# Two graph layers on one core: head projection by seven block products for each pair of node tiles, adjacency in six parts per tile

## The chip, the cores and the metric

The kernel runs on one core of one Trainium2 chip. The metric is the device time of one execution in microseconds. Five engines are named as the profile names them: PE (matrix multiply; PEld is its weight load), DVE (vector), ACT (scalar), POOL and SP (here mostly issuers of transfers).

## The reference

A graph with 3327 nodes and 1024 features per node goes through two layers. Between the two stands a residual sum and a layer norm, and the second layer begins with a projection of every node onto eight heads of 64 features.

```
h = relu(layernorm(x));  x = x + gnn0(h, adj)     # adj @ quantised(relu(quantised(h) @ quantised(w)))
h = relu(layernorm(x));  x = x + gnn1(h, adj)

def gnn1(x, adj):
    Wh = einsum('nf,hfd->hnd', x, W)              # the projection of the heads: [3327 x 1024] @ [1024 x 512]
    e_src, e_dst = Wh . a1, Wh . a2
    att = softmax(where(adj > 0, leaky_relu(e_src + e_dst), -9e15))
    h = elu(att @ Wh)
    return mlp(h)                                 # four dense layers
```

## The kernel before

The nodes are padded to T = 26 tiles of 128. The kernel runs through stages. Stage 1 makes the quantised support `s_int` of the first layer. Stage 2 multiplies the adjacency by it and prepares the second layer for each node tile. Stage 3 is the attention (masks, selections, sums), and stage 4 the dense layers. The change lies in stage 2.

**What stage 2 does for one tile t.** The transposed adjacency of the tile, 26 blocks of 128 by 128, comes in from memory in four parts of 7, 6, 7 and 6 blocks (`SUBS`, used as `PARTS`, lines 47 and 48). For each part the function `adjacency` (line 177) loads `at` (L186, on SP's queue), lets ACT round it to `hi` (L190), lets DVE take the rest as `lo` (L194), and lets DVE write the mask bytes `mk` (L195). There are three buffers for `at`, and two each for `hi` and `lo`; a buffer of `hi` or `lo` comes free when PE has finished the part that used it two parts before. Then PE multiplies each block of `hi` and of `lo` by the support block, in two matmuls of 512 columns each (L723), so a block takes four matmuls and a tile 104. All of them add up in one pair of PSUM banks, `mm`.

When a tile is summed, what follows is called its **row chain** here: ACT scales `mm` into `y` (L738), DVE scales it again (L739), adds the residual row `xt` (L740) and takes the layer norm (L146 to L151); ACT writes two halves `yh` (L616), two transposing transfers turn them (L618, on SP's queue), and ACT joins them to `ht` (L622), the transposed rows of the tile.

**The heads.** `heads(t, ht, r)` (line 645) multiplies `ht` by the head weights `whead` in eight full-precision matmuls of 512 columns (L652), which the profile records as sixteen. ACT takes the sum out of PSUM as `wht` (L659). What comes after that is called the **closing** of a tile here: DVE multiplies and reduces `wht` for both attention vectors (L666, L667), writes two small tables (L670, L671), ACT takes exponentials (L672, L692), DVE scales `ft` (L693, twice), ACT casts `ft` to `fw` (L697), DVE subtracts (L698), ACT casts again (L699), DVE subtracts again (L700), and POOL's queue sends `fw` to memory as `feat_d` (L703). `wht`, `prod`, `ft` and `fw` have one buffer each.

**The order.** In the loop at line 709 the heads of tile t - 1 are called ahead of the last part of tile t. The next part's `adjacency` is always traced one part ahead, at the moment PE's matmuls of a part are traced. So in the text of the program the closing of tile t - 1 stands before the row chain of tile t, and that stands before the casts of parts 1, 2 and 3 of tile t + 1. A scheduler puts the instructions of each engine in order when the program is built; `keep_in_program_order` fixes an instruction behind the one traced before it on its engine, `issue_after` fixes a transfer behind another. The transfer of a tile's first part is issued after the transposes of the tile two before it. The heads of the last two tiles are taken after the loop (line 760 and on), where the attention has begun.

The attention scores of the sources are collected in `srcs` and sent out in batches after the tiles named in `BATCHES` (line 50).

Of the kernel before, what the change touches and what calls it, by code (L numbers as in the profile page):

```python
# [8 lines left out]
F32 = mybir.dt.float32  # L9
# [37 lines left out]
SUBS = [range(0, 7), range(7, 13), range(13, 20), range(20, 26)]  # L47
PARTS = SUBS
GROUPS = [(0, 1), (2, 3), (4, 5), (6,), (7, 8), (9, 10), (11, 12)]
BATCHES = {12: 0, T - 3: 13}  # L50
GT = 2
# [15 lines left out]
def two_layer_kernel(  # L67
# [105 lines left out]
    with tc.tile_pool(name="at", bufs=2, reuse_waits="tile") as atp:  # L173
# [3 lines left out]
        def adjacency(t, js, mk, turned):  # L177

            nj = len(js)
            r = slice(js[0], js[0] + nj)  # L180
            at = atp.tile([P, 7, P], F32, tag="at", name="at", bufs=3)[:, :nj]
            if mk is None:
                mk = atp.tile([P, T + 2, P], U8, tag="mk", name="mk")[:, :T]

            with tc.issue_after(turned.ins) if js is PARTS[0] and turned is not None else nullcontext():
                ins = nc.sync.dma_start(at, adj_t[t][:, r, :])  # L186
            if t == 0:
                tc.keep_in_program_order(ins)
            hi = atp.tile([P, 7, P], F32R, tag="hi", name="hi")[:, :nj]
            ins = nc.scalar.copy(hi, at)  # L190
            if t == 0:
                tc.keep_in_program_order(ins)
            lo = atp.tile([P, 7, P], F32R, tag="lo", name="lo")[:, :nj]
            nc.vector.tensor_tensor(lo, at, hi.bitcast(F32), ALU.subtract)  # L194
            ins = nc.vector.tensor_scalar(mk[:, r], at, 0.0, float(EDGE), ALU.is_gt, ALU.mult)  # L195
            if t == 0:
                tc.keep_in_program_order(ins)
            if js is PARTS[-1]:
                if t == T - 1:
                    nc.vector.memset(mk[:, :, rows_of(t) :], EDGE)  # L200
                nc.gpsimd.dma_start(mask_d[t], mk)
            return hi, lo, mk
# [389 lines left out]

        with tc.tile_pool(name="wh", bufs=1, reuse_waits="tile") as whp, tc.tile_pool(
            name="s2", bufs=2, reuse_waits="tile"
# [5 lines left out]

            whead = whp.tile([P, KF, EMB], F32, name="whead")
            a1_t = whp.tile([P, EMB], F32, name="a1_t")
            a2_t = whp.tile([P, EMB], F32, name="a2_t")

            joins, planes = [], []

            def transposed_by_dma(y):


                ht = s2.tile([P, KF, P], F32, name="ht", bufs=1)  # L610
                parts = []
# [18 lines left out]

            def transposed_by_tensor(y):

                ht = s2.tile([P, KF, P], F32, name="ht", bufs=1)
                ends, copies = [], []
                for g in range(KF // 4):
                    tp = last_ps.tile([P, 4, P], F32, tag="last", name="tp2")
                    turns = [
                        nc.tensor.transpose(tp[:, q, :], y[:, (4 * g + q) * P : (4 * g + q + 1) * P], ident)
                        for q in range(4)
                    ]  # L640
                    ends.append((turns[0], turns[-1]))
                    copies.append(nc.scalar.copy(ht[:, 4 * g : 4 * g + 4, :], tp))
                return ht, ends, copies

            def heads(t, ht, r, own=None):
                if t == T - 1:
                    whm = last_ps.tile([P, EMB], F32, tag="last", name="whm")
                else:
                    whm = wh_ps.tile([P, EMB], F32, name="whm")
                of_k, products, own_lows, own_ups = [], [], [], []  # L650
                for k in range(KF):
                    ins = nc.tensor.matmul(  # L652
                        whm, ht[:, k, :], whead[:, k, :], start=(k == 0), stop=(k == KF - 1)
                    )
                    of_k.append(ins)
                    if k == 0 and t < T - 1:
                        tc.keep_in_program_order(ins)
                wht = s2.tile([P, EMB], F32, name="wht", bufs=1)
                ins = taken = nc.scalar.activation(wht, whm, AF.Copy, scale=r)  # L659
                if t < T - 2:  # L660
                    tc.keep_in_program_order(ins)
                src = srcs[:, t]
# [10 lines left out]
                if t in BATCHES:  # L673
# [5 lines left out]
                    )  # L679
                    srct = s2.tile([P, P], F32, name="srct")  # L680
                    nc.scalar.copy(srct[:n], sp[:n, :P])
# [9 lines left out]
                for q, slope in enumerate((1.0, SLOPE)):  # L691
                    powers.append(nc.scalar.activation(ft[:, :, q, HD], dst, AF.Exp, scale=slope))  # L692
                    scaled = nc.vector.tensor_tensor(  # L693
                        ft[:, :, q, :HD], wh3, ft[:, :, q, HD:].to_broadcast([P, NH, HD]), ALU.mult
                    )
                fw = s2.tile([P, NH, 2, 3, HC], BF16, name="fw", bufs=1)
                highs = nc.scalar.copy(fw[:, :, :, 0], ft)  # L697
                nc.vector.tensor_tensor(ft, ft, fw[:, :, :, 0], ALU.subtract)  # L698
                nc.scalar.copy(fw[:, :, :, 1], ft)  # L699
                lows = nc.vector.tensor_tensor(fw[:, :, :, 2], ft, fw[:, :, :, 1], ALU.subtract)  # L700
                if own is not None:
# [3 lines left out]
                )  # L705
                return of_k, products, lows, powers, highs, taken

            before = None
            for t in range(T):
                xt = s2.tile([P, F], F32, name="xt2")  # L710

                with tc.issue_after(turned.ins) if turned is not None else nullcontext():
                    load_rows(xt, x, t)
                mm = mm_ps.tile([P, F], F32, tag="mm", name="mm2")
                for js in PARTS:
                    hi, lo = part
                    part = next(columns, None)
                    if js is PARTS[-1] and before is not None and t < T - 1:
                        heads(*before)
                    for q, j in enumerate(js):  # L720
                        for which in (hi, lo):
                            for c in range(FC):
# [5 lines left out]
                                    stop=(j == T - 1 and which is lo),  # L728
                                )
                if t == 0:  # L730
                    for dst, ap in (
# [13 lines left out]
                if t == T - 1:  # L745
                    break
                ht, turned = transposed_by_dma(y)
                before = t, ht, r
            supp.close()
# [9 lines left out]

            of_k, products, _, powers, _, taken = heads(*before, own=f_even)  # L760
            queue_behind(products[0], lacking)
            queue_behind(taken, lacking)
            ht, turns, copies = transposed_by_tensor(y)
            queue_behind(copies[0], taken)
# [504 lines left out]
```

## Time and profile before

| what | us |
|---|---|
| median of 3 runs | 2133.86 (2132.22 to 2136.22) |
| the profiled execution | 2132.73 |
| its span in the profile | 2131.0 |
| PE busy in the span | 2096.3 (98%) |
| DVE busy / ACT busy | 1395.4 (65%) / 1343.1 (63%) |
| matmuls of the heads (L652), busy | 182.7 |
| matmuls of the adjacency (L723, hi and lo), busy | 426.3 + 416.8 |

The span is what the profiler sees from the first to the last instruction; the execution took 1.7 us more. Busy times of matmuls overlap, since matmuls are pipelined; the pace of PE is read from the starts, not from these sums. The stretch from about 127 to 899 us is stage 2, from about 983 to 1838 us the attention runs without a break, and the dense layers follow.

In one full tile of stage 2 (564.99 to 595.44 us, 30.45 us long) PE is busy 30.45 us, DVE 17.66 and ACT 15.66.

### The profile page before, as it was taken

What the parts mean: (1) busy time and instruction counts of PE and PEld (TensorE: products, weight loads), DVE (VectorE), ACT (ScalarE), POOL (GpSimd) and SP (SyncE); (2) the same over time, 40 slices, a digit from 0 to 9 for tenths busy, and PEclk for the clock granted to TensorE, in tenths of its full rate; (3) what the DMA queues carried; (4) which work ended last, traced back from release to release, by engine and by line L of the source; (5) the groups of instructions that cost most, each with busy time, mean ns of one, the idle gap of its engine ahead of it and who ended that gap; (6) DMA issues with size and microseconds to landing.
All of it is one profiled execution on the core that took longest, in us unless ns stands there. A gap on an engine that the chain in (4) does not pass through costs nothing.

```text
span 2131.0 us, 36616 instructions
## 1 busy us (share of the span) xinstructions
PE 2096.3 (98%) x15099; PEld 1689.4 (79%) x15109; DVE 1395.4 (65%) x2568; ACT 1343.1 (63%) x1748; POOL 160.7 (8%) x250
## 2 busy tenths in 40 slices
PE   5999999999999999999999999999999999999999
PEld 2467777777777777779999999999999999844444
DVE  8845566556655665577777777777777777655446
ACT  6734454545454545579888888888888888742321
POOL 2300000000200000200000000000000000000000
PEclk9999999999999999999999999999999999999999
DMA  6654544454455444691202012120202104443322
GB/s 219 173 167 142 161 135 147 150 162 135 146 153 161 133 146 153 173 325 26 74 17 74 22 43 57 26 67 21 74 25 75 26 17 132 111 117 119 113 85 74
DMA packets 184088, 233.22 MB, mean 109 GB/s; under 512 B 103924, under 2 KB 132164, under 8 KB 183920
## 3 DMA queue, kind: packets, MB, share of 16 engines
q1 hardware_dynamic: 168684, 176.91, 27.7%
q0 software_dynamic: 15168, 53.90, 8.2%
q8 instruction: 118, 1.93, 0.4%
q14 instruction: 50, 0.41, 0.1%
q10 hardware_dynamic: 68, 0.06, 0.0%
HBM read 141.21 MB, written 66.02 MB: 97 GB/s over the span
## 4 chain that ended last, share of the span: by engine, by line
PE 92%; ACT 2%; DVE 2%; DMA 2%; issue 2%; SPq 0%; POOL 0%; DVEq 0%; POOLq 0%; ACTq 0%
PE acc L875 41%; PE mm L723 28%; PE whm L652 8%; PE o L1179 7%; PE h_ps L1111 5%; PE mm L342 3%; ACT over L846 1%; DMA feat_d<-fw 1%; PE h_ps L1037 1%; DMA xqt<-xq 0%; DMA w<-in_w 0%; DVE stats L255 0%; ACT xb L314 0%; DMA xt<-in_x 0%; DVE w_stats L385 0%
## 5 line engine op out<-in xcount | busy, mean ns | idle before, releaser
L875 PEld LDWEIGHTS <-sel 128*128 128x128 fp8e4 x10816 | 932.1, 97 | 5.9 <-issue 4.6
L846 ACT ACTIVATE over<-srow,large_dst 128x896 uint8<-128x896 f32 (+1 forms) x766 | 684.4, 975 | 30.0 <-DVE sel L855 30.0
L875 PE MATMUL acc<-f_even,sel 128*128 128x195 bf16 x5408 | 468.2, 248 | 0.6 <-DVE su L894 0.5
L875 PE MATMUL acc<-f_odd,sel 128*128 128x195 bf16 x5408 | 467.4, 247 | 0.0
L723 PE MATMUL mm<-s_int,hi 128*128 128x512 f32 x1352 | 426.3, 396 | 0.0
L723 PE MATMUL mm<-s_int,lo 128*128 128x512 f32 x1352 | 416.8, 390 | 0.0
L855 DVE TENSOR_TENSOR sel<-over,mask 128x448 uint32<-128x448 uint32 (+1 forms) x416 | 243.9, 586 | 216.4 <-ACT over L846 115.2
L723 PEld LDWEIGHTS mm<-s_int,hi 128*128 128x128 f32 x1352 | 254.0, 188 | 62.3 <-issue 11.5
L723 PEld LDWEIGHTS mm<-s_int,lo 128*128 128x128 f32 x1352 | 253.8, 188 | 52.8
L856 DVE TENSOR_TENSOR sel<-sel,mask 128x448 uint32<-128x448 uint32 (+1 forms) x416 | 246.0, 591 | 14.2
L190 ACT CAST hi<-at 128x896 fp32r<-128x896 f32 x104 | 92.4, 888 | 152.9 <-PE mm L723 73.3
L652 PE MATMUL whm<-whead,ht 128*128 128x512 f32 x416 | 182.7, 592 | 0.0
L195 DVE TENSOR_SCALAR mk<-at 128x896 uint8<-128x896 f32 (+1 forms) x104 | 59.5, 590 | 172.9 <-DMA at<-in_adj_t 172.8
L194 DVE TENSOR_TENSOR lo<-at,hi 128x896 fp32r<-128x896 f32 x104 | 106.2, 1021 | 68.1 <-ACT hi L190 68.1
L652 PEld LDWEIGHTS whm<-whead,ht 128*128 128x128 f32 x416 | 78.9, 190 | 89.0 <-issue 87.1
L923 POOL DMA_DIRECT2D enc_d<-eh x64 | 57.7, 905 | 860.4 <-ACT eh L921 859.8
L908 ACT ACTIVATE ht<-su,rs 128x64 f32<-128x64 f32 x208 | 53.1, 335 | 108.7 <-DVE rs L904 108.7
L894 DVE TENSOR_REDUCE su<-acc 128x130 f32<-128x390 f32 x208 | 115.7, 556 | 7.9 <-PE acc L875 7.9
L1121 ACT ACTIVATE h<-h_ps,rest 128x512 f32<-128x512 f32 (+1 forms) x52 | 33.7, 654 | 118.7 <-PE h_ps L1111 118.7
L342 PE MATMUL mm<-w_int,xqt 128*128 128x512 bf16 x406 | 93.9, 385 | 6.8 <-DVE w_int L473 4.5
L659 ACT ACTIVATE wht<-whm,lnr 128x512 f32<-128x512 f32 x26 | 17.8, 685 | 119.3 <-PE whm L652 104.5
L622 ACT COPY ht<-yht 128x1024 uint16<-128x1024 uint16 x50 | 67.4, 1356 | 32.3 <-DMA yht<-yh 32.1
(189 smaller groups left out, 1683.5 us busy)
## 6 DMA issues: line engine op xcount, KB each, us to landing
at<-in_adj_t SPq DMA_DIRECT2D x52, 448.0 KB, 4.7
feat_d<-fw POOLq DMA_DIRECT2D x26, 780.0 KB, 6.5
at<-in_adj_t SPq DMA_DIRECT2D x52, 384.0 KB, 4.0
x_d<-xt POOLq DMA_DIRECT2D x26, 512.0 KB, 2.9
nodes<-x_d SPq DMA_DIRECT2D x26, 512.0 KB, 4.9
xt<-in_x SPq DMA_DIRECT2D x25, 512.0 KB, 4.0
out<-yo SPq DMA_DIRECT2D x50, 256.0 KB, 2.0
xs<-in_x SPq DMA_DIRECT2D x24, 512.0 KB, 4.5
```

The lines of the kernel that those rows point to most:

```text
L190: ins = nc.scalar.copy(hi, at)
L194: nc.vector.tensor_tensor(lo, at, hi.bitcast(F32), ALU.subtract)
L342: nc.tensor.matmul(mms[t][:, r], xqts[t][:, k, :], w_int[:, k, r], start=(k == 0), stop=(k == KF - 1))
L652: ins = nc.tensor.matmul(whm, ht[:, k, :], whead[:, k, :], start=(k == 0), stop=(k == KF - 1))
L723: nc.tensor.matmul(mm[:, c * 512 : (c + 1) * 512], which[:, q, :], s_int[j][:, c * 512 : (c + 1) * 512], start=(j == 0 and which is hi), s ...
L846: nc.scalar.activation(over[:, q], srows[i], AF.Relu, bias=large_dst[:, j, h : h + 1], scale=BIG)
L855: pin(nc.vector.tensor_tensor(up, over, of_pair, ALU.bitwise_and))
L856: ends["vector"] = pin(nc.vector.tensor_tensor(dn, up, of_pair, ALU.bitwise_xor))
L875: ins = nc.tensor.matmul(accs[i, b][:, r], chosen[i, pair][:, s, b, q], f[:, j, r], start=(j == 0 and s == 0), stop=(j == T - 1 and s == 1),)
L894: nc.vector.tensor_reduce(su[:, b], accs.pop((i, b)).rearrange("p (q s c) -> p q c s", q=2, s=3), AX.X, ALU.add)
L1111: ins = nc.tensor.matmul(pss[m][:, :cols], wt[:, k, m * P : (m + 1) * P], xt[:, k, :cols], start=(k == 0), stop=(k == k_n - 1),)
L1179: nc.tensor.matmul(ps, st[:, k, q // 2], mv[:, k], start=(k == 0), stop=(k == 1))
```

## The change

For 24 of the 26 tiles the projection is taken for two tiles at once. The rows of the two tiles are seen as a 2 by 2 matrix of blocks (tile, half of the features), the weights as a 2 by 2 matrix of blocks (half of the features, half of the heads). The product of the two is formed from seven products of blocks instead of eight, with sums and differences of blocks before and after. Each block product is four matmuls of 256 columns.

- `weight_differences` makes three difference blocks and overwrites the block `b12` of `whead`; it runs once, in tile 1. Near the end `b12` is loaded again for the last two tiles, which still use eight products.
- `combined` forms the sums and differences of the rows of a pair, in four DVE instructions of 512 columns. It runs in every even tile t from 2 on, for tiles t - 2 and t - 1.
- `pair_of_heads` is a generator: it runs in the last part of that even tile, and puts the products between the four blocks of that part: products 1 and 2, block, 6 and 3, block, 7 and 5, block, 4, block. ACT copies the first product, DVE adds up the others, and then the closings of both tiles follow, one after the other. In odd tiles there is no projection.
- The old closing becomes the function `closing_of_heads`; its instructions are the same.
- The adjacency of a tile comes in six parts of 5, 5, 4, 4, 4 and 4 blocks. The buffers of `at`, `hi` and `lo` keep their numbers (3, 2, 2) and shrink from seven blocks to five.
- `ht` gets two buffers by name (`ht0`, `ht1`). `xt2` goes from two buffers to one. The combined rows use the buffers of `y` and `prod`; `srct` uses that of `prod`. The batches of source scores close one tile later and at the same last tile as before (`BATCHES`).

```
-PARTS = SUBS
+PARTS = [range(0, 5), range(5, 10), range(10, 14), range(14, 18), range(18, 22), range(22, 26)]
+PN = len(PARTS[0])
-BATCHES = {12: 0, T - 3: 13}
+BATCHES = {13: 0, T - 3: 14}
...
+            def weight_differences():
+                for d, one, other in ((t3, b22, b12), (b12, b12, b11), (t2, b22, b12), (t4, b21, t2)):
+                    nc.vector.tensor_tensor(d, one, other, ALU.subtract)
+
+            def combined(t):
+                (a11, a12), (a21, a22) = halves(t), halves(t + 1)
...
+                nc.vector.tensor_tensor(s1, a21, a22, ALU.add)
+                nc.vector.tensor_tensor(s2_, s1, a11, ALU.subtract)
+                nc.vector.tensor_tensor(a21, a11, a21, ALU.subtract)
+                nc.vector.tensor_tensor(s4_, a12, s2_, ALU.subtract)
...
+            def pair_of_heads(t, of):
+                r0, r1 = scales.pop(t), scales.pop(t + 1)
+                wht = s2.tile([P, EMB], F32, name="wht", bufs=1)
...
+                def product(b):
+                    st, mv = of[b]
+                    if b in "1674":
+                        banks.append(wh_ps.tile([P, 2, EMB // 2], F32, name="products"))
+                    ps = banks[-1][:, b in "235"]
+                    for k in range(KF // 2):
+                        order(
+                            nc.tensor.matmul(ps, st[:, k], mv[:, k], start=(k == 0), stop=(k == KF // 2 - 1))
+                        )
+                    return ps
...
+                order(nc.scalar.copy(p1, product("1")))
+                plus(wht[:, half[0]], p1, product("2"))
+                yield
+                plus(u2, p1, product("6"))
+                plus(wht[:, half[1]], u2, product("3"))
+                yield
+                plus(p1, u2, product("7"))
+                of_5 = product("5")
+                plus(wht[:, half[1]], wht[:, half[1]], of_5)
+                yield
+                of_4 = product("4")
+                nc.scalar.activation(wht, wht, AF.Copy, scale=r0)
+                closing_of_heads(t, wht)
+                wht = s2.tile([P, EMB], F32, name="wht", bufs=1)
+                plus(wht[:, half[1]], p1, of_5)
+                plus(wht[:, half[0]], p1, of_4)
+                nc.scalar.activation(wht, wht, AF.Copy, scale=r1)
+                closing_of_heads(t + 1, wht)
+                yield
...
             for t in range(T):
-                xt = s2.tile([P, F], F32, name="xt2")
+                xt = s2.tile([P, F], F32, name="xt2", bufs=1)
...
-                for js in PARTS:
+                paired = t >= 2 and t % 2 == 0
+                steps = iter(())
+                for n, js in enumerate(PARTS):
                     hi, lo = part
                     part = next(columns, None)
-                    if js is PARTS[-1] and before is not None and t < T - 1:
-                        heads(*before)
+                    if t == 1 and n == 0:
+                        weight_differences()
+                    if paired and n == 3:
+                        of = combined(t - 2)
+                    if paired and js is PARTS[-1]:
+                        steps = pair_of_heads(t - 2, of)
                     for q, j in enumerate(js):
+                        next(steps, None)
...
+                if t == T - 2:
+                    nc.gpsimd.dma_start(
+                        b12, w_heads[: F // 2, EMB // 2 :].rearrange("(k p) e -> p k e", p=P)
+                    )
```

## The prediction, made before the changed kernel was run

> **What bounds the kernel now.** First view: the chain of waits in order of time (start, length, what). In stage 2 every piece is PE's:
>
> ```profile
> 686.80 6.87 PE whm L652 x16
> 693.67 23.59 PE mm L723 x104
> ...
> 2086.10 3.45 PE h_ps L1111 x16
> ```
>
> A tile takes 23.59 us for 104 adjacency matmuls (0.2268 each) and 6.87 us for the heads (16 records of 0.429). The two pieces follow each other without a gap, so in this stage each microsecond of PE work taken out is a microsecond of the kernel, as long as nothing else comes late. The last row is from the dense layers, where the last group has two tiles: the same full-precision matmul, but 256 columns wide, at 0.2156 us a record. It is the price of the new products.
>
> Second view: the timelines of ACT and DVE over one tile (start, length, engine, line), to see how much "late" there is room for. Tile t ends at 699.11 (693.67 + 24 x 0.2268); I call that S.
>
> ```profile
> 693.70 0.69 ACT L659 ACTIVATE wht<-whm,lnr 128x512 f32<-128x512 f32 x1 [4.81 <-PE whm L652]
> ...
> 698.75 0.84 ACT L190 CAST hi<-at 128x768 fp32r<-128x768 f32 x1 [1.12 <-issue]
> ```
> ```profile
> 694.42 0.69 DVE L666 TENSOR_TENSOR prod<-wht,a_t 128x512 f32<-128x512 f32 x1 [0.57 <-ACT wht L659]
> ...
> 699.62 0.96 DVE L194 TENSOR_TENSOR lo<-at,hi 128x768 fp32r<-128x768 f32 x1 [0.76 <-ACT hi L190]
> 700.59 1.24 DVE L698 TENSOR_TENSOR ft<-ft,fw 128x1040 f32<-128x1040 f32 x1
> 701.75 0.81 DVE L739 TENSOR_SCALAR y<-y,every,sup_delta 128x1024 f32<-128x1024 f32 x1
> 702.59 1.22 DVE L740 TENSOR_TENSOR xt<-xt,y 128x1024 f32<-128x1024 f32 x1
> 703.73 1.23 DVE L700 TENSOR_TENSOR fw<-ft,fw 128x1040 bf16<-128x1040 f32 x1
> 704.88 1.28 DVE L146 BATCH_NORM_STATS2 stats<-xt 128x6 f32<-128x512 f32 x2
> 706.08 1.07 DVE L194 TENSOR_TENSOR lo<-at,hi 128x896 fp32r<-128x896 f32 x1
> ```
>
> The closing starts 5.4 us ahead of S. The `lo` of part 1 of the next tile is done at S + 1.5, that of part 2 at S + 8.0. PE asks for them at S + 6.35 and S + 11.8 (7 and 13 blocks of 0.907). Room: 4.9 and 3.8 us. Everything DVE owes to the closing and the row chain is over at S + 9.0 (708.13). That is the margin which the change spends.
>
> Third view: ACT at the start of stage 2, to see who goes first when several are ready:
>
> ```profile
> 156.58 1.05 ACT L616 COPY yh<-y 128x1024 uint16<-128x1024 uint16 x1 [4.50 <-DVE y L149]
> 157.53 0.20 ACT L136 ACTIVATE lns<-lnv 128x1 f32<-128x1 f32 x1
> 157.64 1.03 ACT L616 COPY yh<-y 128x1024 uint16<-128x1024 uint16 x1
> 158.57 0.94 ACT L190 CAST hi<-at 128x896 fp32r<-128x896 f32 x1
> ```
>
> Tile 0 ended at 150.6 (its matmuls begin at 127.02), its successor's part 0 at 157.0, so the cast of part 2 could have begun then; it went last, behind everything of tile 0, which stands ahead of it in the program. I take this as the rule: what is traced earlier goes first if it is ready.
>
> **What the Trainium skill says.** "PSUM — Partial Sum Buffer", section "Engine vs sequencer instructions": the queues of ScalarE, VectorE and GpSimdE are strict FIFO, so a waiting instruction holds all behind it. The trace agrees: near the end of stage 2 ACT stood 5.34 us for the landing of `feat_d`, with ready work behind it:
>
> ```profile
> 942.03 1.07 ACT L697 CAST fw<-ft 128x1040 bf16<-128x1040 f32 x1 [5.34 <-DMA feat_d<-fw]
> 943.00 1.97 ACT L846 ACTIVATE over<-srow,large_dst 128x896 uint8<-128x896 f32 x2
> ```
>
> "FP8 and Floating Point Precision", section "TensorE Precision Notes": true fp32 takes four passes. It agrees: 2 x 0.429 us for 512 full-precision columns against 0.227 for the reduced kind. "VectorE: DVE Perf Modes", section on the TRN2 errata: each op pays a fixed cost beside its elements. It agrees for `lo`: 1083 ns at 896 elements, 958 at 768, so 0.98 ns an element and some 0.21 us fixed.
>
> **The change part by part.**
>
> *PE.* Before, a pair takes 32 records of 0.4293 = 13.74 us. After: 7 products x 4 matmuls x 2 records x 0.2156 = 12.07 us. Saved 1.67 us a pair, 20.0 us over 12 pairs. A weight load of 190 ns goes with each record; it still fits under 216, as the last row of the first fence shows. A sure gain on PE.
>
> *Six parts.* Two more each of `hi`, `lo`, `mk` per tile, at fixed shares of about 0.18, 0.21 and 0.16 us (from 896 against 768 elements): 0.2 us of ACT, 0.7 of DVE a tile, beside 23.6 us of PE. Two more transfers on SP's queue, some 0.4 us of issue each, also covered. What costs is the shorter runway: the parts last 4.54, 4.54, 3.63, 3.63, 3.63, 3.63 us instead of 6.35 and 5.44.
>
> *Differences and sums.* `combined`: 4 x 0.69 = 2.8 us of DVE in the even tile; it needs `ht` of the odd tile (before at S + 17.4 with 1.36 us copies) and is done near S + 20.5; product 6 needs it 3.5 + 0.9 us after the last part starts at S + 19.96. Covered, by some 4 us. Seven additions of 256 columns, 0.42 us each by the slope, and one ACT copy. The PSUM bank of products 7 and 4 is that of a product pair two steps back, 4.4 us old; covered. `weight_differences`: 4 x 1.22 = 4.9 us of DVE ahead of tile 1's part 2; with 5 us of row chain beside it, it may cost PE up to 2.8 us once. I take 2.
>
> *`xt2` with one buffer.* Its load waits for the store of the row before (2.9 us to landing, begun at S + 5) and stands behind the transposes on SP's queue at S + 10 anyway. Nothing.
>
> *`b12` again.* One 512 KB load on POOL's queue in tile 24, needed a whole tile later. Nothing.
>
> *The closings, moved and doubled: the term that decides.* Count back from S of an even tile: block 0.91, product 4 1.73, block 0.91. Product 5 ends at S - 3.5; the addition, then ACT's `wht`, and the first closing's `prod` starts at S - 2.2 (before S - 4.7), with a second closing right behind it. All of that and the row chain of tile t stand in the program ahead of the `lo` of part 2 of the odd tile. DVE's bill ahead of that `lo`, from the rows of the table of groups:
>
> - last addition of the first tile 0.42; two additions of the second 0.84
> - closing one: 4 x 0.69 + 0.33 + 2 x 0.69 + 1.24 + 1.23 = 6.9
> - closing two up to its small tables: 4 x 0.69 + 0.33 = 3.1 (its `ft` waits for an exponential of ACT, a moment in which the `lo` slips in)
> - row chain to L151: 0.81 + 1.22 + 1.36 + 0.20 + 0.75 + 0.15 = 4.5
> - `lo` of part 1: 0.83. Its cast is released 0.4 us before S (before at 698.75 too) and it gets in at S + 0.6, when the closing waits for its own reductions and no row is ready. PE wants it at S + 4.54: in time.
>
> Sum 16.6 us from S - 3.4, with about half a microsecond of waits: S + 13.8, and the `lo` itself 0.71: S + 14.5. PE asks at S + 9.07. In between there is no slot, since three chains (closing one, closing two, row chain) alternate and one of them is always ready. So PE stands 14.5 - 9.1 = 5.5 us in each odd tile from 3 to 25: 12 x 5.5 = 66 us.
>
> After that nothing more is late: `lo` of part 3 waits in the same queue and follows at once; the transposes move from S + 10 to about S + 14 and 17, the next tile's first part lands at S + 23.5 and PE, itself late, wants it at S + 29. In even tiles only the row chain competes, and the `lo` of part 2 is done by S + 7.
>
> *The end.* Tile 23's `feat_d` and the source batch leave later in tile 25; SP's loads for the attention stand behind. Between 0 and 6 us; I take 2.
>
> Sum on the profiled execution (span 2131.0 and 1.7 around it): 2132.7 - 20.0 + 66 + 2 + 2 = 2182.7. The median of the runs lies 1.1 us higher than that execution: 2184. The unknown is the wait in odd tiles: at least 0 (the `lo` goes first), at most 10 (two parts starve), which gives 2115 to 2237.
>
> **Rivals.**
> 1. *The gain is kept.* The `lo` of part 2 gets a slot near S + 7, while closing one waits for ACT's second cast and closing two for its `wht`. For it: 706.08, where a `lo` slipped in ahead of L148, which was traced earlier. Against: rows of tile t are ready in that gap. Price 0, time 2132.7 - 20 + 0 to 4, plus 1.1: about 2115. This is the other side; it decides if the `lo` is done by S + 9.1.
> 2. *ACT is held instead.* `fw` has one buffer, so closing two's first cast waits for closing one's `feat_d`: sent at S + 9.1, 0.9 of issue, 6.5 to landing, S + 16.5. If the cast is queued ahead of part 4's `hi` (free at S + 12.3), that is done at S + 18.2 and its `lo` at S + 18.9, against S + 16.33: 2.6 us a pair, 31 in all: 2149. For it the 5.34 us above; against it, that ACT's order may put the cast later. It decides from a landing after S + 14.
> 3. *Worse.* Part 1 starves too (10 us a pair), or PE's clock drops in the gap: "TensorE: Matmul & The Clock Gate", Part 1, gives half clock for some 3.4 us after about as long an idle time; I estimate 1.7 us more a stall, 20 in all. No row of this trace shows it; stage 2 has no such gap. 2204 to 2240.
>
> **How the numbers follow.** Forecast 0.45 (2160 to 2205 for waits of 3.5 to 7 us), rival 1 0.30 (2112 to 2122), rival 2 and shorter waits of 1.5 to 3 us 0.15 (2131 to 2160), rival 3 0.10. Slower by over 0.2% is the forecast, rival 3 and most of rival 2; I put rival 2's low end at 0.03 no change and 0.02 faster: 0.65, 0.03, 0.32. (0.2%, 4.3 us, is about what a measurement of this kernel can tell.) Rival 3 and a little of rival 1 stay outside 2113 to 2204; the likeliest case alone has 2160 to 2205.
>
> **What would show it.** The chain has a piece of some 5 us in odd tiles that is DVE's (L194, or the closing's lines) between 20 and 44 matmuls of L723; products at 0.216 us a record, 12.07 a pair; DVE busy without a gap from S - 2 to S + 14. Wrong if PE runs through odd tiles in 23.6 us, or if the releaser is ACT's `hi` or a transfer.

## The result, and the profile after

| | before | after |
|---|---|---|
| median of 4 runs each, us | 2133.37 (2132.22 to 2136.22) | 2240.35 (2235.01 to 2245.17) |
| span of the profiled execution, us | 2131.0 | 2243.4 |
| stage 2, first to last adjacency matmul, us | 778.9 | 881.2 |
| PE waits of over 0.1 us in stage 2, summed, us | 0 | 74.8 |
| PE at half clock in stage 2, us | 0 | 71.7 |
| a product-free tile / a tile with products, us | 23.57 / 30.45 | 29 to 34 / 36 to 42 |

The changed kernel is slower by a ratio of 1.0499 (95% interval 1.047 to 1.0528). Stage 2 accounts for 102.3 us of the 112.4 us between the spans, and the passage from there into the attention for the other 10. (Counted to its last adjacency matmul, stage 2 before ends at 905.6 us, not at about 899 as given above.)

Parts are counted from 0 here: a tile has parts 0 to 5. The first view of after is the chain of waits in order of time (start, length, what), over the end of tile 14 and the odd tile 15, which begins at 629.74. Before, this chain held nothing but PE.

```profile
627.24 1.73 PE products L700 x8
628.97 0.47 PE mm L813 x2
629.51 0.73 ACT hi L191
...
638.96 1.14 DVE fw L783
640.10 0.60 DVE prod L749
640.82 0.57 DVE lo L195
641.45 6.77 DMA at<-in_adj_t
648.24 0.43 DVE mk L196
649.38 1.21 DVE ft L776 x2
650.62 1.08 ACT fw L780
...
652.88 0.70 DVE lo L195
653.62 17.67 PE mm L813 x68
```

For 24 us the chain leaves PE. It runs through the closings on DVE to the `lo` of part 2, from there through the transfer of part 5, which could begin only when that `lo` had let go of its `at` buffer, then through the `mk` of part 5, and on through the second closing to the next casts. PE's own timeline shows the two places in the tile where it stands (the wait and its releaser are in brackets):

```profile
641.43 0.72 PE L813 MATMUL mm<-s_int,lo 128*128 128x512 f32 x2 [1.99 <-DVE lo L195]
...
652.25 1.22 PE L813 MATMUL mm<-s_int,hi 128*128 128x512 f32 x2 [3.60 <-ACT hi L191]
```

The first wait, for the `lo` of part 2, is 1.99 to 2.0 us in all twelve odd tiles. The second, for the `hi` of part 4 (in tile 25 for its `lo`), is 0.85 to 4.71 us. Here is how they come about. First DVE's timeline:

```profile
640.02 0.68 DVE L749 TENSOR_TENSOR prod<-wht,a_t 128x512 f32<-128x512 f32 x1
640.62 0.20 DVE L149 BATCH_NORM_AGGREGATE mv<-stats 128x2 f32<-128x12 f32 x1
640.74 0.64 DVE L195 TENSOR_TENSOR lo<-at,hi 128x512 fp32r<-128x512 f32 x1
...
644.41 0.41 DVE L196 TENSOR_SCALAR mk<-at 128x512 uint8<-128x512 f32 x1
644.74 0.16 DVE L753 TENSOR_SCALAR ndst<-dst 128x8 f32<-128x8 f32 x1
644.82 0.16 DVE L754 TENSOR_SCALAR large_dst<-dst 128x8 f32<-128x8 f32 x1
648.24 0.43 DVE L196 TENSOR_SCALAR mk<-at 128x512 uint8<-128x512 f32 x1 [3.26 <-DMA at<-in_adj_t]
...
649.30 1.28 DVE L776 TENSOR_TENSOR ft<-wht,ft 128x512 f32<-128x512 f32 x2
```

From 628.26 on DVE has closing one, the start of closing two and most of the row chain ahead of the `lo` at 640.74, whose `hi` was done at 634.70. Then, at 644.9, an `mk` stands at the head of DVE's queue although its block of the adjacency has not landed, and for 3.26 us holds what stands behind it: four small instructions of the row chain and the `ft` of closing two, for which the exponentials were there at 647.0. ACT's timeline shows who needs that `ft`:

```profile
634.08 0.62 ACT L191 CAST hi<-at 128x512 fp32r<-128x512 f32 x1 [1.12 <-issue]
...
646.69 0.32 ACT L775 ACTIVATE ft<-dst 128x8 f32<-128x8 f32 x2
646.91 1.03 ACT L620 COPY yh<-y 128x1024 uint16<-128x1024 uint16 x1
648.83 1.33 ACT L626 COPY ht<-yht 128x1024 uint16<-128x1024 uint16 x1 [0.89 <-DMA yht<-yh]
650.62 1.07 ACT L780 CAST fw<-ft 128x1040 bf16<-128x1040 f32 x1 [0.46 <-DVE ft L776]
651.59 1.13 ACT L191 CAST hi<-at 128x512 fp32r<-128x512 f32 x2
```

The two `hi` that PE wants, of parts 4 and 5, stand behind an `fw` of closing two. They stand behind more than that: PE asks at 648.65, and ACT's queue has the exponentials, a `yh` and an `ht` of the row chain ahead of them, which waits for its transposes until 648.83. The `fw` itself waits only 0.46 us for the held `ft`. So the second wait is again mostly order, this time on ACT, and the hold lengthens it. PE itself is slower afterwards. The windows view (stretch, its length, busy time of PE, PEld, DVE, ACT and POOL, then the granted clock, the DMA share and GB/s) splits the time around the second wait:

```profile
641.43:652.25 10.82, 7.22 (x31) 5.61 (x31) 6.32 (x17) 8.38 (x13) 3.29 (x7) 0.94 0.97 190
652.25:656.00 3.75, 3.60 (x8) 2.40 (x9) 2.99 (x4) 2.64 (x3) 2.04 (x5) 0.50 0.92 316
656.00:659.50 3.50, 3.50 (x13) 2.80 (x12) 1.64 (x5) 0.73 (x1) 3.30 (x6) 0.75 0.27 84
659.50:663.00 3.50, 3.50 (x17) 2.86 (x17) 0.68 (x1) 0.76 (x2) 0.00 (x0) 1.00 0.88 255
```

After the wait the clock is 0.50, and it is back at 1.00 only 7 us later: 8 and 13 matmuls in the second and third stretch against 17 in the fourth.

The sum, by tile lengths: the twelve odd tiles take 381.2 us where twelve bare ones at 23.57 would take 282.8, so +98.4. Of that, 26.8 us were lost in 129 spaces from one matmul's start to the next that passed at half clock with no wait in them. The other 71.6 belong nearly all to the waits, of which the table's column counts 60.6: it counts from the modelled end of a matmul, 0.16 us later than the pace of 0.2268 us, and leaves out those below 0.1 us. (Of the 64.9 us at half clock in these tiles, 10.7 lie in spaces with a wait in them, where the clock costs less or nothing.) The twelve even tiles take 451.6 against 12 x 35.94 without a wait: +20.3. The products themselves bring 12 x (2 x 30.45 - 35.94 - 23.57) = 16.7 us. That is 102.0 of the 102.3 us.

### The profile page after: what moved, and what is told of

Same layout as the page of the kernel before. It is cut to its first block, busy times and chain, and to the rows that moved or that the text cites. A ratio compares the mean times of both kernels' runs of the same rounds, so it can differ in the third digit from the quotient of the medians.

```text
span 2243.4 us, 37763 instructions
## 1 busy us (share of the span) xinstructions
PE 2127.5 (95%) x15387; PEld 1760.1 (78%) x15397; DVE 1458.2 (65%) x2808; ACT 1351.4 (60%) x1812; POOL 161.8 (7%) x251
## 4 chain that ended last, share of the span: by engine, by line
PE 71%; DVE 10%; DMA 9%; ACT 6%; issue 3%; SPq 0%; POOL 0%; DVEq 0%; ACTq 0%; POOLq 0%
PE acc L969 39%; PE mm L813 12%; PE o L1273 7%; DMA at<-in_adj_t 6%; PE products L700 5%; PE h_ps L1205 5%; PE mm L343 3%; DMA yht<-yh 2%; DVE lo L195 1%; DVE ft L776 1%; ACT over L940 1%; DVE stats L147 1%; DVE xt L834 1%; ACT L755 1%; DVE ft L781 1%
## 5 line engine op out<-in xcount | busy, mean ns | idle before, releaser
L813 PE MATMUL mm<-s_int,lo 128*128 128x512 f32 x1352 | 448.6, 410 | 33.4 <-DVE lo L195 32.6
L813 PE MATMUL mm<-s_int,hi 128*128 128x512 f32 x1352 | 443.9, 410 | 33.0 <-ACT hi L191 33.0
L813 PEld LDWEIGHTS mm<-s_int,lo 128*128 128x128 f32 x1352 | 261.2, 195 | 101.8 <-DVE lo L195 47.8
L813 PEld LDWEIGHTS mm<-s_int,hi 128*128 128x128 f32 x1352 | 262.9, 195 | 94.1 <-ACT hi L191 39.2
L191 ACT CAST hi<-at 128x640 fp32r<-128x640 f32 (+1 forms) x156 | 100.7, 653 | 196.9 <-PE mm L813 171.4
L196 DVE TENSOR_SCALAR mk<-at 128x512 uint8<-128x512 f32 (+1 forms) x156 | 70.4, 456 | 141.8 <-DMA at<-in_adj_t 141.1
L195 DVE TENSOR_TENSOR lo<-at,hi 128x640 fp32r<-128x640 f32 (+1 forms) x156 | 112.1, 724 | 76.4 <-ACT hi L191 73.9
L718 ACT ACTIVATE wht<-wht,lnr 128x512 f32<-128x512 f32 x12 | 8.7, 722 | 149.1 <-DVE wht L705 149.1
L343 PEld LDWEIGHTS <-xqt 128*128 128x128 bf16 x416 | 40.5, 99 | 55.3 <-issue 8.8
L620 ACT COPY yh<-y 128x1024 uint16<-128x1024 uint16 x50 | 51.9, 1038 | 43.0 <-DVE y L150 43.0
```

Of the source, the lines that this page charges most:

```text
L343: nc.tensor.matmul(mms[t][:, r], xqts[t][:, k, :], w_int[:, k, r], start=(k == 0), stop=(k == KF - 1))
L813: nc.tensor.matmul(mm[:, c * 512 : (c + 1) * 512], which[:, q, :], s_int[j][:, c * 512 : (c + 1) * 512], start=(j == 0 and which is hi), s ...
```

## Experiments

Three theories were named in the expectations. *Order*: PE waits because the casts stand in DVE's and ACT's queues behind two closings and a row chain. *Hold*: it waits because `mk`, waiting for its transfer, holds DVE's queue. *Parts*: it waits because six short parts give too little lead. The first four kernels test one thing each.

**Six parts alone.** The kernel before with the six parts; its buffers stay at seven blocks.

```
-PARTS = SUBS
+PARTS = [range(0, 5), range(5, 10), range(10, 14), range(14, 18), range(18, 22), range(22, 26)]
```

> The kernel before with the adjacency in six parts and nothing else of the change (eight products, one projection and one closing a tile, buffers of the old size and number). Theory 'order' (two closings and a row chain queued ahead of the casts are what stalls PE): a tile has only one closing, so PE stays near full; 2133 to 2160 us. Theory 'parts' (the shorter parts alone leave too little time between the release of a buffer and its need): most of the loss is here already, above 2200 us. Theory 'hold' (DVE stands at a mask instruction that waits for its transfer): some of it, 2150 to 2190 us.

Measured: 2143.25 us, ratio 1.0042 (1.0028 to 1.0057). Stage 2 grows by 4.6 us with no wait over 1.07 us, the passage to the attention by 5. That is in the range given for *order*. *Parts* by itself is worth 9 of the 107 us. Whether the shorter parts also make the doubled closing worse is open: the changed kernel with the four old parts was not run.

**The second closing moved.** One more `yield` ends the even tile's work after closing one; closing two, with its last two additions, is traced in the odd tile ahead of the matmuls of its fourth part, part 3 as counted here (the expectations of the runs count parts from 1).

```
                 closing_of_heads(t, wht)
+                yield
...
+                    if t % 2 and n == 3:
+                        next(steps, None)
```

> The changed kernel with the second closing of a pair moved into the odd tile, ahead of its fourth part; everything else as changed. Theory 'order': the two closings no longer stand in one queue, the waits of PE in odd tiles fall under 1 us a pair and the clock stays whole; 2113 to 2140 us. Theory 'parts': the waits stay, above 2190 us. Theory 'hold': the first wait of an odd tile (2 us) goes, the second (3 us) stays in part; 2150 to 2190 us.

Measured: 2180.55 us, ratio 1.0215 (1.02 to 1.0231). Most odd tiles take 23.8 to 24.1 us: both their waits are gone, and the clock drops with them. (Tiles 9 and 11 keep 0.8 and 0.9 us, and tile 15 waits 2.3 us for `srcs`.) Most even tiles take 38 to 39 us and three about 42, with waits of 0.3 to 2.7 us, mostly for `lo`; `mk` waits up to 5.65 us for its transfer there. So undoing the doubled queue takes away 60 of the 107 us. The time lies in the range given for *hold*, not in the one for *order*, but the waits that are left are not the ones named there: they have moved into the even tiles.

**Casts ahead.** The order of tracing is overruled for the two casts only.

```
-            ins = nc.scalar.copy(hi, at)
+            with tc.high_priority():
+                ins = nc.scalar.copy(hi, at)
...
-            nc.vector.tensor_tensor(lo, at, hi.bitcast(F32), ALU.subtract)
+            with tc.high_priority():
+                nc.vector.tensor_tensor(lo, at, hi.bitcast(F32), ALU.subtract)
```

> The changed kernel with the casts to hi and lo given the highest priority when the order of each engine is drawn up; everything else as changed, both closings still in a row. Theory 'order': a cast then waits for one instruction at most, both waits of the odd tiles go; 2113 to 2140 us. Theory 'parts': no effect on the wait, above 2190 us. Theory 'hold': the first wait goes, the second stays where DVE or ACT stand for a transfer; 2150 to 2190 us.

Measured: 2204.92 us, ratio 1.033 (1.0313 to 1.0347). No wait is left inside the odd tiles from 3 on, but each even tile from 4 on now begins with one, of 2.9 to 3.9 us, for the `hi` of part 0. The time is as high as *parts* would have it, but for another reason. The casts went ahead as meant, and the row chain came late: its transposes start 16.2 and 20.4 us into the odd tile (tiles 11 and 17) where they started at 14.0 and 18.1 before this edit, and the first transfer of the next tile, which is tied to them, lands some 3 us after PE has run out of work.

**mk behind lo.** Each `mk` is queued behind the `lo` of its own part.

```
-            nc.vector.tensor_tensor(lo, at, hi.bitcast(F32), ALU.subtract)
+            low = nc.vector.tensor_tensor(lo, at, hi.bitcast(F32), ALU.subtract)
             ins = nc.vector.tensor_scalar(mk[:, r], at, 0.0, float(EDGE), ALU.is_gt, ALU.mult)
+            queue_behind(ins, low)
```

> The changed kernel with each mask instruction of DVE queued behind the lo of its own part, so that DVE never stands at a mask instruction for a transfer; everything else as changed. Theory 'hold': the second wait of the odd tiles (3 us and the clock that falls after it) goes; 2160 to 2195 us. Theory 'order': the cast of part 5 still queues on ACT behind the exponentials, the second yh, the first ht and the fw cast of the second closing; 2205 to 2240 us. Both leave the first wait of 2 us.

Measured: 2205.04 us, ratio 1.0326 (1.0311 to 1.0341). All twelve even tiles take 35.94 us. In the odd ones the first wait stays at 1.99 to 2.04 us. The second falls from 32.9 to 18.5 us over the stage: it is gone or at most 1.2 us in seven tiles and 2.2 to 3.8 in five. So *hold* is what delays the even tiles and less than half of the second wait, and has no part in the first. What stays of the second wait is the order on ACT, here in tile 9, where PE waits 1.23 us until 428.90 and the `fw` no longer waits for a held `ft`:

```profile
426.05 1.35 ACT L627 COPY ht<-yht 128x1024 uint16<-128x1024 uint16 x1 [0.71 <-DMA yht<-yh]
427.27 1.06 ACT L781 CAST fw<-ft 128x1040 bf16<-128x1040 f32 x1
428.24 1.13 ACT L191 CAST hi<-at 128x512 fp32r<-128x512 f32 x2
```

The time, 2205.04, is at the low end of the range for *order*.

The other four combinations of these three edits complete the table.

> The changed kernel with two of the edits tried so far at once: the second closing moved to the odd tile, ahead of part 4, and each mk queued behind the lo of its part. If order and hold are two causes that add up (the first stall of the odd tiles is order and goes with the closing, the waits left in the even tiles are mk holding VectorE's queue and go with the queueing), the odd tiles take 23.9 us, the even ones 35.9, together 59.9 against 60.9 before, the half clock of stage two falls below 5 us, and the median is 2120 to 2140. If the even tiles' waits in the run with the closing moved alone are order (lo behind the first closing), they stay at 38 to 39 us and the median stays at 2170 to 2185.

> The changed kernel with the second closing moved to the odd tile, ahead of part 4, and hi and lo cast ahead of other work. If order is the whole cause, lo no longer stands behind a closing anywhere, the even tiles take 35.9 us, the odd ones 23.9, and the median is 2115 to 2135. If hold is the rest, mk ahead of its transfer still keeps VectorE's queue while the row chain that is put back by the casts lets the transfers start late, the stage keeps 1.5 to 3.5 us of wait a pair with the half clock behind it, and the median is 2165 to 2200.

> The changed kernel with all three edits: second closing moved, casts ahead, mk behind lo. If the three causes add up, it is the fastest of the three of this call, 2115 to 2135, with stage two's half clock below 5 us. If the casts ahead do harm of their own by putting back the row chain, whose turned rows come late for the products (transposes at 697.9 to 702 us where the changed kernel has them earlier), it is 10 us or more above the run with the closing moved and mk behind lo.

> The last of the eight combinations of the three edits: casts ahead and mk behind lo, both closings left together. The run with all three was 10 us above the kernel before, each edit alone 46 to 71 above. If the stalls are the queueing of the casts alone (behind closings and behind a waiting mk) and the place of the second closing is of no account once both are undone, it is 2140 to 2155, within 10 us of the run with all three. If the doubled closing costs by itself, by the row chain that it puts back (its turned rows late for the products), the odd tiles keep a wait and the median is 2170 to 2200.

| second closing moved | casts ahead | mk behind lo | us | ratio to before |
|---|---|---|---|---|
| no | no | no | 2240.35 | 1.0499 |
| yes | no | no | 2180.55 | 1.0215 |
| no | yes | no | 2204.92 | 1.033 |
| no | no | yes | 2205.04 | 1.0326 |
| yes | no | yes | 2177.65 | 1.02 |
| yes | yes | no | 2186.84 | 1.0247 |
| no | yes | yes | 2210.4 | 1.035 |
| yes | yes | yes | 2145.93 | 1.0054 (1.0039 to 1.0069) |

Two of the four expectations missed: with all three edits the time is above the 2115 to 2135 us of causes that add up, and casts ahead with `mk` behind `lo` is above both of its ranges. With the closing moved and `mk` behind `lo` the time fell where `lo` behind closing one would put it, but the waits left in the even tiles are for `hi`. The edits don't add up. The three single gains are 60, 35 and 35 us; all three together bring 94. With the second closing moved, either of the other two alone brings almost nothing (-3 and +6 us), and both bring 35. What each leaves open is seen in its timeline. With the closing moved and `mk` behind `lo`, ACT at the end of an even tile's first half:

```profile
309.12 1.05 ACT L621 COPY yh<-y 128x1024 uint16<-128x1024 uint16 x1 [5.20 <-DVE y L150]
310.18 1.28 ACT L137 ACT_TABLE_LOAD   x1
311.47 0.20 ACT L137 ACTIVATE lns<-lnv 128x1 f32<-128x1 f32 x1
311.58 1.03 ACT L621 COPY yh<-y 128x1024 uint16<-128x1024 uint16 x1
312.52 0.61 ACT L191 CAST hi<-at 128x512 fp32r<-128x512 f32 x1
```

The `hi`, of part 3, goes last, behind the whole row chain, though ACT had stood idle until 309.12 and PE had finished with the buffer (that of part 1) at about 307.6: PE waits 1.56 us at 313.18. With all three edits the `hi` of part 3 goes ahead of the table load and starts 8.9 us into the even tile (613.43 in tile 16) instead of 14.1, and the even tiles take 35.9 to 36.5 us.

Casts ahead and `mk` behind `lo`, with both closings left together, is the combination that shows what the doubled closing does. SP's queue, ACT and PE at the border of tiles 11 and 12:

```profile
499.13 6.50 SPq L625 DMA_TRANSPOSE yht<-yh  x2
505.73 0.70 SPq L132 DMA_DIRECT2D xt<-in_x  x1
506.52 13.43 SPq L187 DMA_DIRECT2D at<-in_adj_t  x6
```
```profile
511.25 1.56 ACT L192 CAST hi<-at 128x640 fp32r<-128x640 f32 x2 [0.96 <-DMA at<-in_adj_t]
```
```profile
512.03 1.22 PE L816 MATMUL mm<-s_int,hi 128*128 128x512 f32 x2 [5.37 <-ACT hi L192]
```

Now the casts are in time and the row chain is late. Its transposes go out 16 us and more into the odd tile (which began at 482.93). The first transfer of the next tile is tied to them (`issue_after(turned.ins)`) and lands 5 us too late. Each even tile starts with 4.3 to 8.3 us of wait, and the clock drops after it. From the start of tile 11 to these transposes, 16.20 us, DVE is busy for 15.67; then ACT stands 1.89 us for the transfer of a `hi` that now goes ahead of the second `yh` (503.27). In the four kernels with both closings together either the casts or the row chain came late, and PE waited in each. Untying the next tile's first transfer from the transposes, which is how the late row chain reaches PE, was not tried.

**What the three edits leave.** PE's waits from 100 to 1000 us in the run with all three (total, times, longest):

```profile
PE sp L764 <- DVE srcs L754: 5.4, 2, 2.7
PE whm L738 <- ACT ht L629: 5.1, 1, 5.1
PE mm L820 <- ACT hi L192: 4.9, 5, 1.5
```

Half of it is near the end (5.1 us for `ht`, and one of the two waits for `srcs`): closing two of tiles 22 and 23 falls into tile 25. In the next kernel these two tiles are projected one by one as before the change, in tiles 23 and 24, and the batches of source scores close where they closed then.

```
-                paired = t >= 2 and t % 2 == 0
+                paired = 2 <= t < T - 2 and t % 2 == 0
...
+                    if js is PARTS[-1] and t in (T - 3, T - 2):
+                        heads(t - 1, hts[t - 1], scales[t - 1])
...
-                if t == T - 2:
+                if t == T - 4:
                     nc.gpsimd.dma_start(
```

> The three edits, and tiles 22 and 23 projected one by one as in the kernel before, in the last parts of tiles 23 and 24 (the column block of the weights is read again after tile 22), so that no second closing falls into tile 25. If what the three edits leave is mostly the end (in that run: 2.7 us of wait for the turned srcs and 3.4 us at half clock in tile 25, then 5.1 us of wait for ht, whose transposes stood behind the last mk on the queues, 14.4 us from the last adjacency product to the first of stage three against 9.6 before), some 10 us go, less 1.4 us for the pair that gains nothing, and the median is 2134 to 2139. If the end is late for another reason, 2143 to 2148.

Measured: 2143.67 us, ratio 1.004 (1.0027 to 1.0052), no better than the run with all three within the spread (2139.92 to 2146.69 here). Tile 25 takes 23.57 us and stage 2 never loses its clock, but `whm` still waits 4.7 us for `ht`: SP's queue has

```profile
901.85 0.33 SPq L913 DMA_DIRECT2D srow<-src_d  x1
902.23 5.57 SPq L625 DMA_TRANSPOSE yht<-yh  x2
```

where the `yh` was done at 898.6. The `srow` load begins right after the last `mk` (901.35 and 0.42 long), and the transposes stand behind it. On ACT the `ht` then stands behind an `over` that waits for that `srow` (907.00, 3.84 us long), and starts at 910.75, 1.85 us after the first transpose had landed.

**Two tries on the rest.** First, the joining of an even tile's rows (`ht` on ACT) traced after the `hi` of the odd tile's last part.

```
+                    if t % 2 and n == 4 and t < T - 4:
+                        joined(ht, turns)
```

> The same, and the joining of an even tile's turned rows (ht on ScalarE) put into the next tile's fifth part, behind the hi of its last part, instead of ahead of it. If the waits left in the odd tiles (0.5 to 1.6 us, once with 3.4 us of half clock) are hi behind an ht that waits for its transposes, they go, some 10 us with the clock, and the median is 2122 to 2132, faster than both kernels. If hi is then late behind something else, the same as the other run within 2 us.

Measured: 2154.08 us, ratio 1.0091 (1.0075 to 1.0106). The odd tiles become clean as expected (0.72 us of waits in all), and the even ones get the waits instead: 37.0 to 40.5 us each. In tile 18 the `ht` of tile 17 now waits 3.42 us on ACT for its transposes, and the `hi` behind it costs PE 1.84 us; why those transposes are late was not followed up.

Second, the transposes ahead of `srow` at the end, and the same with seven smaller parts and a third buffer of `hi`.

```
-        queue_behind(planes[0], load_src(0))
+        queue_behind(load_src(0), planes[-1])
...
-        queue_behind(joins[0], ends["scalar"])
+        queue_behind(ends["first"], joins[1])
```

> The kernel with the last pair projected one by one, and at the end the transposes of tile 24 ahead of the first srow load on SP's queue, with the joining of ht ahead of the first over on ScalarE. There srow waited for the last mk until 901.85 and held the transposes, whose yh was there at 898.6, and whm then waited 4.7 us for ht. If that is the end's cost, whm starts at once and the median is 3 to 5 us lower, 2138.5 to 2141; if over and sel then come later by as much, it stays at 2143 to 2145.

Measured: 2155.45 us, ratio 1.0095 (1.0081 to 1.0109), a miss by some 15 us. ACT and PE in tile 25:

```profile
913.74 1.33 ACT L629 COPY ht<-yht 128x1024 uint16<-128x1024 uint16 x1 [13.79 <-DMA yht<-yh]
914.94 0.60 ACT L192 CAST hi<-at 128x512 fp32r<-128x512 f32 x1
```
```profile
915.60 1.22 PE L822 MATMUL mm<-s_int,hi 128*128 128x512 f32 x2 [10.47 <-ACT hi L192]
```

The transposes went out at 897.0 and the first result came 16.7 us later. Five mask loads of POOL's queue (issued at 897.1 to 899.8) and the loads that now followed on SP's queue at once (from 904.6 on) were under way beside them; which of them delayed the result was not tried. And with `ht` no longer tied behind `over`, it was queued ahead of the last `hi`. The old tie of `ht` to `over` had kept it out of that place.

```
-PARTS = [range(0, 5), range(5, 10), range(10, 14), range(14, 18), range(18, 22), range(22, 26)]
+PARTS = [range(0, 4), range(4, 8), range(8, 12), range(12, 16), range(16, 19), range(19, 22), range(22, 26)]
...
+            hi = atp.tile([P, PN, P], F32R, tag="hi", name="hi", bufs=3)[:, :nj]
```

> The same with seven parts of three or four blocks, at and hi in three buffers each and lo in two, 32 blocks of room where there were 35. If what the odd tiles still wait (4.4 us in all in gaps, and some 0.5 us a tile that shows as no gap) is hi waiting for its buffer with only one part of 3.6 us cast ahead, it goes: the odd tiles take 23.7, the even ones 36.0, and the median is 2127 to 2135, at or below the kernel before. If the smaller parts only add casts and transfers on queues that are late anyway, it is 2140 or above.

Measured: 2204.69 us, ratio 1.0318 (1.0297 to 1.034). The even tiles begin with waits of 0.9 to 3.5 us again, and ACT's `hi` waits 49.3 us in all for its transfers from 170 to 880 us (10.6 us in the run ahead of it). It carries the end of that run too, so some 12 us of its 61 over the kernel with the last pair alone belong there. A third `hi` buffer with larger parts wasn't tried.

No version was found that beats the kernel before. The nearest, at ratio 1.004, has the 16.7 us of products less one pair's share, and has lost it to short waits in stage 2 (780.6 us against 778.9) and to the passage at the end (first attention matmul 13.2 us after stage 2's last, against 6.8 before).

## Why the prediction was right or wrong

The direction was right, and so was the first part of the mechanism: the doubled closing starves the odd tiles. The time was 36 us above the range's upper end. By its steps:

- *PE.* A pair's products were to take 12.07 us; the tile with products shows 35.94 - 23.57 = 12.37, and the saving is 16.7 us for the 20.0 of the text. The price of 0.2156 us a record holds inside a product; the 0.3 us a pair are the changes between products and blocks (1.73 to 1.82 us for eight records in the chain).
- *Six parts.* "Covered": 9 us in the run that has nothing else. A small error.
- *Differences.* Tile 1 takes 24.56 us, 1.0 more than a bare tile, for 2 of the text.
- *The closings, moved and doubled.* **This is the step that failed**, in the sentence "After that nothing more is late". The bill of 16.6 us ended in one stall of 5.5 us a pair. In the trace the first stall is 1.99 us: the bill counted the end of the row chain and the rest of closing two's tables ahead of the `lo` of part 2, and that `lo` got in between, at S + 11.0 for S + 13.8. But a second stall follows, for the `hi` of part 4, of 2.7 us on average (32.9 over twelve tiles). It comes through what the text had at nothing. On ACT that `hi` stands behind closing two's exponentials and `fw` and behind the row chain's `ht`. And the late `lo` gives its `at` buffer back late, so a transfer starts late, and an `mk` that waits for it holds DVE and with it the `ft` that this `fw` needs. The run with `mk` behind `lo` took 14.4 of the 32.9 us and left the first stall alone. The two stalls together are 5 us a pair with the short waits beside them, close to the 5.5 of the text by luck: the one forecast is a third of its size, and one that was not forecast makes up for it.
- *The clock.* The text put the halved clock into the third rival, as an estimate of 1.7 us a stall, 20 us in all. It is at most 35.8 us in stage 2 (half of 71.7; in the odd tiles 26.8 of it were counted matmul by matmul). It belonged in the forecast: a stall forecast on PE has this price with it, and the forecast's own waits of 5.5 us were long enough.
- *Even tiles.* "Only the row chain competes" there; they lose 20.3 us, to `u`, `lo` and `hi` behind a held DVE. All of it goes in the run with `mk` behind `lo`, where they take 35.94 us.
- *The end.* 2 us taken, 0 to 6 as bounds; 10 measured. `whm` waits 4.28 us for an `ht` whose transposes stood behind a `srow` load on SP's queue, and which itself stood behind an `over` on ACT until 1010.55, when the first transpose had landed at 1007.83.

So from the forecast: +66 for the stall, and in its place 98.4 in odd tiles with their clock and 20.3 in even ones; -16.7 for -20.0; 1 for 2 for the differences; 10 for 2 at the end. That is 63 us more than the 2182.7 of the text for the profiled execution, which took 2245.2. Of the rivals the first is out. The second had the right place, part 4's `hi` behind an `fw`, and the right size of 2.6 us, but `fw` waited 0.46 us for `ft`, not for `feat_d`. The third came out at the top of its 2204 to 2240, by the clock and by a second starving part, which was part 4 and not part 1. What was left outside the range, a chance of one in ten, should have been inside it.

On what the Trainium skill says: "PSUM — Partial Sum Buffer", section "Engine vs sequencer instructions" (a queue is a strict FIFO), is what *hold* rests on, and the `mk` at 648.24 agrees: DVE stood 3.26 us for it, with the exponentials' result for `ft` there from 647.0.

## What to carry to other kernels

Before moving work to another place on a loaded in-order engine, list every instruction that will stand behind it, and follow each one a step further: the buffer that it frees, the transfer which that starts, and the instruction that waits for that transfer at the head of a queue. An instruction that waits for a DMA should not be ahead of work that is ready. Price a stall of TensorE as the stall and the halved clock after it, and set both against the saving: 16.7 us of matmuls could not pay for a chain that had 3.8 us of room.

## What the runs showed of the hardware

The clock of PE fell only at times that lie on a fixed grid of 3.41 us, for one to four steps of it, after a step in which PE had waited for some half of the time. Taken over the kernels here, of which all but the one before have drops, and their 97 drops in stage 2 and the 40 us after it (worked out from the granted clock and the time in which PE ran nothing): a step at full clock with over 1.9 us of waiting was followed by half clock each time, one with under 1.5 us never, and between them it went both ways. So the same wait of 1.99 us costs a drop in some odd tiles and none in others, as it falls within one step or over two. In the Trainium skill, "TensorE: Matmul & The Clock Gate", Part 1, says that the window is free-running and some 3.4 us long, and the runs agree; it gives a whole idle window as the condition, and here just over half of one (1.9 of 3.41 us) was always enough.

A transfer of 256 KB that takes 2.8 us to land as the median over the run took 6.77 us at 641.45 in tile 15, where `feat_d` (780 KB), a row store, a row load and two transposes were issued within the 16 us around it. The same transfer took 5.5 to 7.8 us in all twelve odd tiles from 3 on. It is what the `mk` waited for; which of the others held it was not tried.
